# More products of ones before norms and inside linear attention, and an earlier first mask, in a twelve-sublayer decoder

## The chip, the core and the metric

The kernel runs on one core of one Trainium2 chip. The metric is device microseconds of one execution. Three executions of the kernel before took 899.19, 896.45 and 893.0 us; their median is 896.45 us.

## What is computed

The reference is a decoder of four layers on x (16 sequences of 64 tokens, 128 features, so 1024 tokens) with a context of the same shape. Each layer has a self-mixing sublayer, a cross attention to the context and a feed-forward sublayer, and each sublayer ends with its input added and a layer norm:

```
x = _layernorm(x + _L0_attn_ref(x, ...))     # linear attention
x = _layernorm(x + _L0_xattn_ref(ctx, x, ctx, mask_BxSx1_ff1, ...))
x = _layernorm(x + _L0_ffn_ref(x, ...))      # local attention and a gated net, twice
x = _layernorm(x + _L1_attn_ref(x, ...))
x = _layernorm(x + _L1_xattn_ref(x, ctx, ctx, ...))
x = _layernorm(x + _L1_ffn_ref(x, ...))      # a net, scaled by two weights
x = _layernorm(x + _L2_attn_ref(x, ...))     # the recurrence
...                                          # xattn, switch; attn, xattn, top-2 experts
```

Linear attention, the first sublayer, makes q, k, v and two gates w and r for 16 heads of 8 features, norms q and k to unit length, and sums over the 64 places s of a sequence's *batch* axis (its input counts the axis of 16 as places and the axis of 64 as batch):

```
A   = einsum('sbnq,sbnv->bnvq', k, v * w)
out = einsum('sbnq,bnvq->sbnv', q, A) * r    # then a projection
```

The recurrence mixes each token with the one before it, projects, applies relu, and runs state = state * decay + h along the 64 tokens, then projects again:

```
inp = mix * x + (1 - mix) * shifted
h = relu(inp @ W_in.T + b_in)
state = state * decay + h                    # along the tokens
out = state @ W_out.T + b_out
```

The mask of the first cross attention lets a query attend to a key only if both have a nonzero entry in mask_BxSx1_ff1.

## The kernel before

All activations stay on the chip. The 1024 tokens are two halves of 512 (h = 0 and 1), each held twice: `xt` with tokens on partitions (4 tiles of 128 by 128), for sums and norms, and `x` with features on partitions (128 by 512), for projections. Names of tiles carry the sublayer: la (linear attention), xa (every cross attention), lb (local attention), at (self attention), sf (the net of layer 1), rc (the recurrence), sw and tt (the experts).

*Order.* The source is written as Python generators: `first_stream(h)` strings the sublayers from the first cross attention (tag xa0) to the third (xa2) together, and `side_by_side` takes turns between half 0, which leads by five steps, and half 1. What the source records is then ordered by a scheduler in the tile layer, which writes one fixed list for each engine; an engine works through its list in order and waits on semaphores. So an instruction that waits holds all behind it on its engine, and the position of an instruction can differ from its place in the source.

*Buffers.* PSUM has a pool of two tiles of two banks (`psc`, tag sc, for scores and la_a) and a pool of four one-bank tiles (`pt`, tag t) for everything else: projections (la_ps, xa_pq, rc_p), transposes (la_o, xa_pt, px), outputs (po, xa_av). A new tile of a tag takes the buffer of the fourth tile before it and must wait until that one's readers are done. SBUF work tiles come from `buf(kb, ...)`, rings of 8 tiles of 2 KB, 7 of 4 KB and 4 of 8 KB per partition.

*Products of ones.* `keep_busy(out)` (L156) multiplies a 128x128 tile of ones in bf16 with 512 columns of ones into a PSUM tile which the next real product overwrites. It has no other effect on the result. It already stands 12 times before the first projection, once before most projections and transposes, four times in the norms of linear attention, six times in local attention, eight times in half 1 of xa2 and xa3.

*Linear attention* (L280 and on). The tokens are taken in eight groups of 128, in four pairs. `front(pair)` projects (la_ps: L286 and the bias rows L293), squares q and k (ACT L297), makes the gates (ACT L302), sums the squares (DVE L298) and takes the inverse root in a chain of small DVE steps (`inverse_root`, L772 to L781). `back(pair)` scales q, k and v into la_four (DVE L314), spreads v (POOL L321), transposes q (PE L333 into la_o, copied by ACT L334), forms k times v (PE L327 into la_a), masks it to its heads (DVE L329 into la_am), multiplies with q (PE L339), copies (ACT L346), transposes back (PE L348) and copies into la_att (ACT L351). front(1) is recorded before back(0), front(2) before back(1), and so on. `project_close` then makes the output projection po_la, adds the residual and calls `close`.

*Norms.* `close` makes the statistics on DVE (L195, L197), the inverse deviation in two POOL steps (L201, L204), the normed xt on DVE (L206), and returns a `flip`, which, when the stream calls it, transposes xt by PE (L224, or L235 for xa0) into px and has ACT copy it to x (L226). Its `ones` says how many products of ones the flip puts in front of its transposes.

*First cross attention.* Keys are masked by POOL (xa_km, L441), base_xa is the residual with the output's bias (POOL L685, L688), scores are PE L480, and where there is a mask, an extra product adds it to the scores (PE L491). Then follow the maximum (DVE L536), the subtraction (DVE L537), the exponent (ACT L540), transposes (PE L551) and the product with the values (PE L572). The mask tile is made by `mask_outer`: two DMAs on SP (L704) bring the mask (mo_m), POOL multiplies it (L709), DVE turns it into large negative numbers in bf16 (mo_b, L710). `attention` makes it when it first needs it:

```
        if mask and tag not in self.masks:
            self.masks[tag] = mask(work)
```

*Net and recurrence.* `sorted_ffn` runs its net for half 0 alone (half 1 only gets the second norm), and `recurrence(h)` makes the mixed input (DVE L1127, L1128), the projection rc_p (PE L151 through `group`), relu (ACT L1134), the scan (DVE L1137), the output projection po_rc (PE L151), the sum (DVE L1144) and the norm. DMA loads are issued by SP in order; w7 and w4, the weights of later cross attentions, are loaded into the places of weights that PE must have finished with.

Of the kernel before, what the change touches and what calls it, by code (L numbers as in the profile page):

```python
# [37 lines left out]
class Kernel:  # L38
# [227 lines left out]
    def linear_attention(self):  # L266


        nc, work, psc, pt = self.nc, self.aw, self.psc, self.pt
        att = self.buf(4, [N], "la_att")  # L270
        att_b = att.rearrange("p (s b j) -> p s b j", b=S // 2, j=2)
        blk8 = self.g("blk8").unsqueeze(1).to_broadcast([P, 8, P])
        pos4 = self.g("pos4").unsqueeze(2).to_broadcast([P, 4, P])

        def front(pair):
            ss = work.tile([P, 2, 32], F32, tag="la_ss", name=f"la_ss{pair}")
            made = []
            for i in range(2):
                gr = pair * 2 + i
                ps = self.psum(pt, f"la_ps{gr}")  # L280

                for _ in range(12 if gr == 0 else 1):
                    self.keep_busy(ps)
                w = self.g("L0a_w")
                n = w.shape[1]
                nc.tensor.matmul(  # L286
                    ps[:, :n], self.x_all[:, bass.ts(gr, P)], w, start=True, stop=False
                )

                rows = [self.la_b] if pair == 0 else la_b3  # L290
                ones = self.g("one") if pair == 0 else self.ones_b
                for row in rows:
                    nc.tensor.matmul(  # L293
                        ps[:, :n], ones[0:1, :], row, start=False, stop=row is rows[-1]
                    )
                sq = self.buf(2, [HALF], f"la_sq{gr}")
                nc.scalar.activation(sq[:, 0:256], ps[:, 0:256], AF.Square)  # L297
                nc.vector.tensor_reduce(  # L298
                    ss[:, i, :], sq[:, 0:256].rearrange("p (n d) -> p n d", d=8), AX.X, ALU.add
                )  # L300
                gates = work.tile([P, 32], F32, tag="la_g", name=f"la_g{gr}", bufs=4)
                nc.scalar.activation(gates, ps[:, 384:416], AF.Sigmoid)  # L302
                made.append((ps, sq, gates))
            return made, self.inverse_root(work, ss.rearrange("p i n -> p (i n)"), f"la_{pair}")

        def back(pair, made, rs):
            for i, (ps, sq, gates) in enumerate(made):
                gr = pair * 2 + i
                four = self.buf(2, [4, P], f"la_four{gr}")
                rq = work.tile([P, 16], F32, tag="la_rq", name=f"la_rq{gr}")  # L310
                nc.vector.tensor_tensor(rq, rs[:, i * 32 : i * 32 + 16], gates[:, 16:32], ALU.mult)
                factors = (rq, rs[:, i * 32 + 16 : i * 32 + 32], gates[:, 0:16])
                for n, by in enumerate(factors):
                    nc.vector.tensor_tensor(  # L314
                        four[:, n, :].rearrange("p (h d) -> p h d", d=8),
                        ps[:, bass.ts(n, P)].rearrange("p (h d) -> p h d", d=8),
                        by.unsqueeze(2).to_broadcast([P, 16, 8]),
                        ALU.mult,
                    )
                vm = sq.rearrange("p (i d) -> p i d", d=P)  # L320
                nc.gpsimd.tensor_tensor(  # L321
                    vm, four[:, 2, :].unsqueeze(1).to_broadcast([P, 4, P]), pos4, ALU.mult
                )
                a = psc.tile([P, 2, HALF], F32, tag="sc", name=f"la_a{gr}")
                for t in range(2):
                    r = slice(64 * t, 64 * t + 64)
                    nc.tensor.matmul(a[:, t, :], four[r, 1, :], sq[r, :], start=True, stop=True)  # L327
                am = self.buf(4, [8, P], f"la_am{gr}")
                nc.vector.tensor_tensor(  # L329
                    am, a.rearrange("p t (i d) -> p (t i) d", d=P), blk8, ALU.mult  # L330
                )
                po = pt.tile([P, 4, P], F32, tag="t", name=f"la_o{gr}")
                nc.tensor.transpose(po[:, 0, :], four[:, 0, :], self.g("ident"))  # L333
                nc.scalar.copy(four[:, 3, :], po[:, 0, :])  # L334

                for m in range(2):
                    for j in range(4):
                        at = (m * 4 + j) // 2 * 32
                        nc.tensor.matmul(  # L339
                            po[32 * j : 32 * j + 32, 1 + m, :],  # L340
                            four[:, 3, at : at + 32],
                            am[:, m * 4 + j, :],
                            start=True,
                            stop=True,
                        )
                nc.scalar.copy(four[:, 0:2, :], po[:, 1:3, :])  # L346
                for m in range(2):
                    nc.tensor.transpose(po[:, 1 + m, :], four[:, m, :], self.g("ident"))  # L348
                to = po[:, 1:3, :].rearrange("p m (a b) -> p m a b", b=64)
                for j in range(2):  # L350
                    nc.scalar.copy(  # L351
                        att_b[:, :, gr * 4 : gr * 4 + 4, j].rearrange("p s (m a) -> p m a s", m=2),
                        to[:, :, :, 48 * j : 48 * j + 16],
                    )
        fronts = [front(0)]
        la_b3 = []
        rows3 = self.lbp.tile([P, 2080], F32, tag="v0", name="la_b3").bitcast(BF16)
        for i in range(3):
            row = rows3[0:1, bass.ts(i, 416)]
            nc.vector.tensor_copy(row, self.la_b)  # L360
            if i < 2:
                nc.vector.tensor_tensor(self.la_b, self.la_b, row, ALU.subtract)
            la_b3.append(row)
        for pair in range(4):
            if pair < 3:
                fronts.append(front(pair + 1))
            back(pair, *fronts[pair])
        return self.project_close(pt, self.g("L0a_wo"), att, "L0a_bo", "la")


# [37 lines left out]
    def attention(  # L408
        self, h, tag, kv, hd, scale, wq, wk, wv, wo, bq=None, bk=None, bv=None, bo=None,
# [4 lines left out]
        work, psc, pt = self.aw, self.psc, self.pt  # L414
# [206 lines left out]
        if wo is not None:  # L621
# [5 lines left out]
            y = self.new_y(tag, h)  # L627
# [6 lines left out]
            else:  # L634
                nc.vector.tensor_tensor(y, ps, base, ALU.add)

        ones = 8 if h == 1 and tag in ("xa2", "xa3") else 1
        flip = self.close(pt, h, y, tag, shift=tag == "xa0", ones=ones)
        yield "last"
        flip()  # L640
# [434 lines left out]
    def sorted_ffn(self, h):  # L1075
# [30 lines left out]
        for i in range(4):  # L1106
            nc.vector.scalar_tensor_tensor(
                y[:, i, :], acc[:, i, :], ws[:, i : i + 1], self.xt[h][:, i, :], ALU.mult, ALU.add
            )
        flip = self.close(pt, h, y, "sf")  # L1110
        yield "last"
        flip()

# [1 line left out]
    def recurrence(self, h):  # L1115
        nc, pt, sc = self.nc, self.pt, self.scalars
        yield
        base = self.base(h, "rc_bout", "rc")
        rest = self.aw.tile([P, 1], F32, tag="rest", name=f"rc_rest{h}", bufs=2)
        nc.vector.tensor_scalar(rest, sc[:, 1:2], -1.0, 1.0, ALU.mult, ALU.add)  # L1120
        dec = self.buf(2, [8, S], f"rc_dec{h}")
        nc.gpsimd.memset(dec, 1.0)
        nc.gpsimd.memset(dec[:, :, 0:1], 0.0)
        nc.gpsimd.tensor_scalar(dec, dec, sc[:, 0:1], 1.0, ALU.mult, ALU.mult)
        inp = self.buf(2, [8, S], f"rc_inp{h}")
        x3 = self.x[h].rearrange("p (b s) -> p b s", s=S)
        nc.vector.tensor_scalar(inp, x3, sc[:, 1:2], None, ALU.mult)  # L1127
        nc.vector.scalar_tensor_tensor(  # L1128
            inp[:, :, 1:S], x3[:, :, 0 : S - 1], rest, inp[:, :, 1:S], ALU.mult, ALU.add
        )  # L1130
        ps = self.psum(pt, f"rc_p{h}")
        self.group(ps, [(self.g("rc_win"), inp.rearrange("p b s -> p (b s)"))])
        hid = self.buf(2, [HALF], f"rc_hid{h}")
        nc.scalar.activation(hid, ps, AF.Relu, bias=self.g("rc_bin"))  # L1134
        yield
        st = self.buf(2, [HALF], f"rc_st{h}")
        nc.vector.tensor_tensor_scan(  # L1137
            st, dec.rearrange("p b s -> p (b s)"), hid, 0.0, ALU.mult, ALU.add
        )
        ps = pt.tile([P, 4, D], F32, tag="t", name=f"po_rc{h}")  # L1140
        for i in range(4):
            self.group(ps[:, i, :], [(st[:, bass.ts(i, P)], self.g("rc_wout"))])
        y = self.new_y("rc", h)
        nc.vector.tensor_tensor(y, ps, base, ALU.add)  # L1144
        flip = self.close(pt, h, y, "rc")
        yield "last"
        flip()

# [846 lines left out]
```

## Time and profile before

| what | value |
|---|---|
| median of three executions | 896.45 us (893.0 to 899.19) |
| the profiled execution | 892.14 us |
| its span, first to last instruction | 890.4 us |
| mean TensorE clock granted | 0.893 of full |
| PE busy | 737.5 us, 83% of the span |
| PE weight loads, beside PE | 467.7 us, 53% |
| DVE busy | 493.2 us, 55% |
| ACT busy | 361.7 us, 41% |
| POOL busy | 264.8 us, 30% |
| products of ones of 512 columns into xa_pt, mean | 390 ns each, 80 of them |

Busy time is the sum of an engine's instructions; matmuls are pipelined, so that a row of them takes less than its number times the mean. The second part of the page cuts the span into 40 equal slices and gives each engine's busy share in tenths, and as PEclk the clock that TensorE was granted, where 9 is full or nearly so. The order in time gives each instruction's start, its duration, its engine and line, what it writes and reads, and in brackets how long the engine had stood idle and what ended that.

### The profile page before, as it was taken

What the parts mean: (1) busy time and instruction counts of PE and PEld (TensorE: products, weight loads), DVE (VectorE), ACT (ScalarE), POOL (GpSimd) and SP (SyncE); (2) the same over time, 40 slices, a digit from 0 to 9 for tenths busy, and PEclk for the clock granted to TensorE, in tenths of its full rate; (3) what the DMA queues carried; (4) which work ended last, traced back from release to release, by engine and by line L of the source; (5) the groups of instructions that cost most, each with busy time, mean ns of one, the idle gap of its engine ahead of it and who ended that gap; (6) DMA issues with size and microseconds to landing.
All of it is one profiled execution on the core that took longest, in us unless ns stands there. A gap on an engine that the chain in (4) does not pass through costs nothing.

```text
span 890.4 us, 17664 instructions
## 1 busy us (share of the span) xinstructions
PE 737.5 (83%) x7145; PEld 467.7 (53%) x7147; DVE 493.2 (55%) x1126; ACT 361.7 (41%) x602; POOL 264.8 (30%) x299
## 2 busy tenths in 40 slices
PE   6777888878777889789978999869767999968990
PEld 2334546455554556457564577536444565735770
DVE  4565466564846656364536575445444456665663
ACT  2223456355455534364713365323215434512320
POOL 2323143260615321212025300146151011017732
PEclk7878989899999999899977899969968799968995
DMA  7700000000000000500000000152106632021102
GB/s 278 242 13 13 1 1 2 13 1 2 1 1 1 2 1 1 190 2 1 1 1 1 1 3 1 43 134 71 49 22 190 190 115 76 14 107 51 54 25 80
DMA packets 35543, 44.43 MB, mean 50 GB/s; under 512 B 7732, under 2 KB 27445, under 8 KB 34824
## 3 DMA queue, kind: packets, MB, share of 16 engines
q1 hardware_dynamic: 33000, 38.26, 13.6%
q0 software_dynamic: 2464, 5.05, 2.0%
q8 instruction: 58, 0.95, 0.4%
q14 instruction: 21, 0.17, 0.1%
HBM read 34.51 MB, written 11.80 MB: 52 GB/s over the span
## 4 chain that ended last, share of the span: by engine, by line
PE 54%; DVE 18%; POOL 7%; ACT 5%; issue 4%; DMA 3%; SPq 1%; DVEq 0%; POOLq 0%; ACTq 0%
PE xa_sc L480 4%; PE xa_av L572 4%; PE xa_pt L551 3%; PE tt_py L151 3%; PE sw_pe L151 3%; PE tt_ph L151 2%; PE at_sc L480 2%; DVE lb_t L818 2%; PE lb_qk L151 2%; DVE lb_t L832 2%; PE at_av L572 2%; PE xa_sc L491 2%; PE at_pt L551 2%; PE xa_pt L156 1%; PE lb_pw L151 1%
## 5 line engine op out<-in xcount | busy, mean ns | idle before, releaser
L536 DVE TENSOR_REDUCE xa_mx<-xa_sc 128x16 f32<-128x1024 f32 x40 | 48.7, 1219 | 63.8 <-PE xa_sc L491 41.3
L838 POOL TENSOR_TENSOR lb_t<-lb_t,lb_t 128x1024 f32<-128x1024 f32 x16 | 37.7, 2357 | 99.4 <-DVE lb_t L832 95.2
L554 ACT COPY xa_eT<-xa_pt 128x512 f32<-128x512 f32 x80 | 45.5, 587 | 40.8 <-PE xa_pt L551 40.0
L540 ACT ACTIVATE xa_e<-xa_e 128x1024 f32<-128x1024 f32 x40 | 42.3, 1058 | 37.6 <-DVE xa_e L537 37.5
L480 PE MATMUL xa_sc<-xa_km,xa_q 32*64 32x256 f32 x640 | 55.2, 404 | 0.7 <-ACT xa_q L431 0.5
L441 POOL TENSOR_SCALAR xa_km<-xa_k,const 128x512 f32<-128x512 f32 x40 | 27.0, 695 | 82.5 <-ACT xa_k L429 49.1
L551 PE MATMUL xa_pt<-const,xa_e 128*128 128x128 f32 x320 | 48.8, 280 | 1.8 <-ACT xa_e L540 1.8
L537 DVE TENSOR_TENSOR xa_e<-xa_sc,xa_mx 128x1024 f32<-128x1024 f32 x40 | 48.7, 1218 | 2.1
L551 PEld LDWEIGHTS xa_pt<-const,xa_e 128*128 128x128 f32 x320 | 40.3, 145 | 13.1 <-ACT xa_e L540 3.7
L572 PEld LDWEIGHTS xa_av<-v,xa_eT 128*64 128x64 f32 x1280 | 40.5, 138 | 8.2 <-issue 6.1
L572 PE MATMUL xa_av<-v,xa_eT 128*64 128x18 f32 (+1 forms) x1280 | 44.2, 209 | 0.0
L156 PEld LDWEIGHTS <-ones_b 128*128 128x128 bf16 x255 | 25.3, 106 | 35.9 <-issue 19.8
L151 PE MATMUL lb_qk<-w,lb_hs 128*128 128x512 f32 x64 | 35.8, 686 | 8.5 <-DVE lb_t L832 4.8
L480 PEld LDWEIGHTS xa_sc<-xa_km,xa_q 32*64 32x64 f32 x640 | 24.7, 136 | 19.9 <-issue 12.8
L201 POOL TENSOR_TENSOR rstd_xa<-mv_xa,eps 128x4 f32<-128x4 f32 x8 | 1.6, 200 | 112.2 <-DVE mv_xa L197 112.2
L814 DVE TENSOR_REDUCE lb_ss<-lb_t 128x16 f32<-128x1024 f32 x16 | 19.5, 1217 | 27.9 <-ACT lb_t L811 27.9
L156 PE MATMUL xa_pt<-ones_b 128*128 128x512 bf16 x80 | 30.2, 390 | 0.0
L862 POOL TENSOR_TENSOR lb_t<-lb_t,lb_rs 128x1024 f32<-128x1024 f32 x16 | 30.1, 1902 | 0.0
L1610 POOL DMA_INDIRECT tt_out<-tt_ys,tt_outs x23 | 22.5, 976 | 18.6 <-DVE tt_ys L1609 16.2
L868 PE MATMUL lb_pf<-const,lb_t 128*128 128x128 f32 x128 | 20.1, 312 | 9.4 <-POOL lb_t L862 9.3
L480 PE MATMUL at_sc<-at_km,at_q 32*64 32x256 f32 x256 | 22.5, 446 | 6.0 <-DVE at_rel L533 4.5
L151 PE MATMUL sw_pe<-sw_gu,sw_xs 128*128 x46 | 26.7, 665 | 0.0
(471 smaller groups left out, 1762.9 us busy)
## 6 DMA issues: line engine op xcount, KB each, us to landing
sw_gu<-in_sw_gu SPq DMA_DIRECT2D x4, 1024.0 KB, 6.8
at_mem<-at_rsb SPq DMA_DIRECT2D x16, 256.0 KB, 2.7
at_rel<-at_mem SPq DMA_DIRECT2D x32, 128.0 KB, 2.9
w<-in_w SPq DMA_DIRECT2D x1, 3114.0 KB, 13.7
sw_dn<-in_sw_dn SPq DMA_DIRECT2D x4, 512.0 KB, 7.0
tt_w<-in_tt_w SPq DMA_DIRECT2D x2, 1024.0 KB, 8.0
tt_b<-in_tt_b SPq DMA_DIRECT2D x1, 2048.0 KB, 7.4
sw_in<-in_zeros SPq DMA_DIRECT2D x1, 1472.0 KB, 11.2
```

Of the source, the lines that this page charges most:

```text
L151: self.nc.tensor.matmul(out, lhsT, rhs, start=n == 0, stop=n == len(pairs) - 1)
L156: self.nc.tensor.matmul(out, self.ones_b, self.ones_b.unsqueeze(1).to_broadcast([P, 4, P]), start=True, stop=True)
L441: nc.gpsimd.tensor_scalar(kms[-1][:, i % 4, :], k, hm[:, i : i + 1], 1.0, ALU.mult, ALU.mult)
L480: nc.tensor.matmul(sc[64 * j : 64 * j + 64, gg, at : at + 256], q[r, t], part[r, :, t] if local else part[r, :, :], start=not masked or (p ...
L536: nc.vector.tensor_reduce(mx, scored, AX.X, ALU.max)
L537: nc.vector.tensor_tensor(e3, scored, mx.unsqueeze(2).to_broadcast([P, 16, S]), ALU.subtract)
L540: nc.scalar.activation(e3, e3, AF.Exp, scale=scale)
L551: nc.tensor.transpose(ps[:, bass.ts(n, P)], blocks[:, bass.ts(n, P)], self.g("ident"))
L554: nc.scalar.copy(eT[:, gg, :], ps)
L572: nc.tensor.matmul(av[64 * j : 64 * j + 64, pr, hp, :, :], eT[:, gg, at : at + 64], v[:, b, hp, :, :], start=True, stop=True,)
L838: nc.gpsimd.tensor_tensor(t1, t1, t2.rearrange("p t n d -> p t (n d)"), ALU.add)
L862: nc.gpsimd.tensor_tensor(t3, t3, rs[:, bass.ts(r, 16)].unsqueeze(2).to_broadcast([P, 16, 64]), ALU.mult)
```

## The change

Products of ones are added in five places, and one call is moved.

- In `back`, before the transpose into la_o: ten in the first group of the first pair, four in the first group of the other pairs, two in the second group of each pair. They are written into the la_o tile.
- The flip of xa0 in half 0 gets four instead of one.
- The flip of sf in half 0 gets four instead of none (`close` in half 1 of `sorted_ffn` is another call and stays at none).
- In the recurrence, before the projection rc_p and before po_rc: six each in half 0, three each in half 1.
- The flip of rc gets four instead of none in both halves.
- `mask_outer` for xa0 is called at the end of the four pairs of linear attention, ahead of `project_close`, instead of in the attention. Its two DMAs, its POOL product and its DVE step go with it. Its tile comes from the ring of 2 KB tiles, so it takes another place in that ring.

```diff
                 po = pt.tile([P, 4, P], F32, tag="t", name=f"la_o{gr}")
+
+                for _ in range((10 if pair == 0 else 4) if i == 0 else 2):
+                    self.keep_busy(po.rearrange("p n m -> p (n m)"))
                 nc.tensor.transpose(po[:, 0, :], four[:, 0, :], self.g("ident"))
...
             back(pair, *fronts[pair])
+
+        self.masks["xa0"] = self.mask_outer(work)
         return self.project_close(pt, self.g("L0a_wo"), att, "L0a_bo", "la")
...
-        ones = 8 if h == 1 and tag in ("xa2", "xa3") else 1
+        ones = 8 if h == 1 and tag in ("xa2", "xa3") else 4 if h == 0 and tag == "xa0" else 1
...
-        flip = self.close(pt, h, y, "sf")
+        flip = self.close(pt, h, y, "sf", ones=4)
...
         ps = self.psum(pt, f"rc_p{h}")
+        for _ in range(6 - 3 * h):
+            self.keep_busy(ps)
         self.group(ps, [(self.g("rc_win"), inp.rearrange("p b s -> p (b s)"))])
...
         ps = pt.tile([P, 4, D], F32, tag="t", name=f"po_rc{h}")
+        for _ in range(6 - 3 * h):
+            self.keep_busy(ps.rearrange("p i d -> p (i d)"))
         for i in range(4):
...
-        flip = self.close(pt, h, y, "rc")
+        flip = self.close(pt, h, y, "rc", ones=4)
```

The change can be built without being run, and the built lists show where the scheduler puts things. In linear attention the ten products stand directly ahead of the first L333; in the later pairs three of the four stand ahead of L327 and one behind it, and in the last pair the two parts of a group's L327 are pulled apart by other products. The POOL step of the mask stands behind the last L321, its DVE step between the last two L329, its DMAs ahead of the load of w7. Around the recurrence of half 0 the lists of PE, DVE and POOL change in order as well: the keys' projection xa_pk and the end of half 1's previous cross attention stand between rc_p and po_rc, and seven of POOL's eight xa_km stand before the inverse deviation of rc, where before it was one.

## The prediction

> **What bounds the kernel now.** I read the busy row and the clock row of the page first, since the change only adds work to TensorE. PE is busy 83% of the span, but the clock row falls under full speed again and again, and the chain that ended last is 54% PE.
>
> ```profile
> ## 2 busy tenths in 40 slices
> PE   6777888878777889789978999869767999968990
> ...
> PEclk7878989899999999899977899969968799968995
> ```
>
> Then I took the clock in 1 us steps. It has two values, 1.00 and 0.50, and changes only at instants 3.413 us apart (10.46, 24.12, 34.36, 37.78, 48.0, 58.26, 78.74, 85.56, 457.62, 467.86 us and so on, all at 0.23 us past a multiple). The table of stages shows the slow stretches in the regions that the change touches; behind the comma stands PE busy, and PEclk is the column before the DMA share.
>
> ```profile
> 10.46:24.11 13.65, 7.60 (x18) 2.62 (x17) 10.54 (x43) 1.59 (x8) 2.40 (x3) 0.50 0.95 352
> 48.01:58.25 10.24, 9.17 (x49) 4.10 (x51) 6.24 (x19) 2.21 (x9) 2.43 (x3) 0.50 0.00 1
> 74.34:77.74 3.40, 0.01 (x2) 0.03 (x1) 0.97 (x4) 1.21 (x1) 2.26 (x2) 1.00 0.01 2
> 78.73:85.56 6.83, 6.83 (x40) 3.07 (x33) 5.51 (x5) 2.26 (x3) 0.00 (x0) 0.50 0.01 2
> 457.62:467.86 10.24, 5.85 (x14) 3.21 (x14) 4.27 (x10) 1.27 (x2) 3.37 (x3) 0.50 0.00 1
> 471.27:478.10 6.83, 6.47 (x39) 3.50 (x39) 3.96 (x13) 1.02 (x2) 6.83 (x11) 0.50 0.00 0
> 501.99:508.82 6.83, 6.57 (x45) 3.48 (x49) 1.88 (x4) 3.59 (x5) 2.69 (x4) 0.50 0.00 0
> ```
>
> Last came the order of time. In these lines: start, duration, instruction; in brackets the idle time ahead of it and its releaser. First the start of linear attention, then the mask, then the recurrence.
>
> ```profile
> 18.64 0.29 DVE L314 TENSOR_TENSOR la_four<-la_ps,la_g 128x128 f32<-128x128 f32 x1
> 19.08 0.45 PE L333 MATMUL la_o<-const,la_four 128*128 128x128 f32 x1 [4.05 <-DVE la_root L781]
> 21.25 3.39 PE L327 MATMUL la_a<-la_sq,la_four 64*128 64x512 f32 x8
> 23.38 2.54 DVE L329 TENSOR_TENSOR la_am<-la_a,const 128x1024 f32<-128x1024 f32 x2 [1.02 <-PE la_a L327]
> ...
> 74.97 1.26 POOL L688 TENSOR_TENSOR base_xa<-base_xa,xt_la 128x512 f32<-128x512 f32 x1 [1.23 <-DVE xt_la L206]
> 76.19 1.04 POOL L709 TENSOR_TENSOR mo_m<-mo_m,cols 128x512 f32<-128x512 f32 x1
> 77.74 0.59 PE L491 MATMUL xa_sc<-mo_b,ident_b 128*128 128x512 bf16 x2 [3.40 <-DVE mo_b L710]
> 80.59 1.06 PE L156 MATMUL xa_pt<-ones_b 128*128 128x512 bf16 x2
> ...
> 460.05 2.05 PE L151 MATMUL rc_p<-rc_inp,w 128*128 128x512 f32 x2 [2.35 <-issue]
> 464.13 2.08 PE L151 MATMUL po_rc<-w,rc_st 128*128 128x128 f32 x8 [2.04 <-DVE rc_st L1137]
> 489.85 1.12 PE L151 MATMUL rc_p<-rc_inp,w 128*128 128x512 f32 x2
> 493.82 1.16 PE L151 MATMUL po_rc<-w,rc_st 128*128 128x128 f32 x8
> ```
>
> The reader is to see three things. PE waits 4.05 us for the first transpose of linear attention. PE stands 3.40 us before the first mask product, because POOL's L709 stands behind two base_xa steps, and the clock then halves for 6.83 us. And the same recurrence product takes 2.05 us in half 0 and 1.12 us in half 1.
>
> **What the Trainium skill says.** "TensorE: Matmul & The Clock Gate", section "Part 1: The HAM clock gate", says that a free-running window of 3413 ns decides between half and full clock, and that idle halves it. The trace agrees: steps of 3.413 us, values 0.50 and 1.00. The same page, "HAM oscillation", asks for no idle gap over about 3.4 us; here a full-speed window that is 0.59 to 0.68 busy sometimes fell (454.2 to 457.6, 0.68) and sometimes not (65.1 to 68.5, 0.59), so I treat about half as the edge. Its "Part 4: PE-mode transpose" says that transposes don't count as busy in the same way, which fits the fall at 457.6 after a window with four transposes.
>
> **Prices.** One product of ones costs 0.216 us at full clock (four took 1.03 with 0.38 for the last: 0.65/3) and 0.43 at half (two took 1.06, the last 0.63). The change adds 30 in linear attention (10+2, then three times 4+2), 3 for xa0, 4 for sf, 12+6+8 for the recurrence: 63.
>
> **Part 1, the mask.** In the built order of the changed kernel its POOL product stands right after the last L321, where POOL idles (9.23 us before 64.59), its DVE step between the last two L329, and its two DMAs (3.4 us from issue to landing) on SP ahead of the loads of w7 and w4, which wait for PE; POOL's base_xa and norm steps are passed only by 1.04 us that ends before their inputs are there. All of that is covered; without the cover it would cost 1.04+0.43. What goes is the stall: L491 can start when the scores end, at 74.34, not 77.74. Next late are DVE and ACT: maximum from 75.0 (DVE has xt_la until 74.9), subtraction to 77.5, exponent 78.6, transposes at full clock from 79.25, second exponent and the copies after it, and the first xa_av at 82.35 against 87.50. That is 5.1 us: 3.4 of stall and 1.7 of half clock. PE is full until 104, so it lasts. I take 4.9 (3.4 to 5.3).
>
> **Part 2, ones in linear attention.** la_o takes the buffer of the first la_ps, since four buffers hold la_ps 0 to 3, so its ten ones can't run in the 4.05 us gap: they start with the wait's end, 19.08, after the L314 of 18.64 has freed it, and at half clock. 10x0.43 = 4.3, to 23.35; transpose 0.45; two ones and a transpose at about full clock 0.8; la_a from 24.6 in place of 21.25, but at full clock 0.9 instead of 1.7 before the first L329, which moves from 23.38 to about 25.6: +2.2. A window that falls otherwise gives 1.6 to 3.1. DVE, ACT and the next projections wait behind it in order, so it is not absorbed. In pairs 1 and 2 the four ones fit PE's waits (1.13 before 32.94, 1.19 and 0.86 around 45.5), and L329 is bound by DVE's root steps, so a faster la_a gains nothing there; the two ones before the next transpose stand ahead of L348 and cost about 0.3. In pairs 2 and 3 full clock instead of the 10.24 us at half would bring the last L329 2.4 us forward, but the order now puts the second la_a product of the last group behind L339 of the group before, which gives 1.4 back, and ones ahead of its transpose another 0.4: -0.6. Sum +2.2+0.3-0.6 = +1.9; if the clock falls again there, +1 more. I take +2.2 (bounds: -3.2, the clock gains of 0.85 and 2.4 with all ones covered; and +12.8, all 30 at 0.43 on the path).
>
> **Part 3, xa0.** Two of the extra ones run before the transposes at 107.7, one or two in the gap after 108.8. lb_qk at 113.79 runs at half clock (3.4 before ACT, 1.7 at full), but the 2.5 us idle just before it stays. I take a quarter of 1.7: -0.4 (0 to -1.7).
>
> **Part 4, sf and recurrence.** In half 0 the ones of sf and rc_p fill 454.5 to 458, the six of po_rc 459.2 to 460.5, so both windows are full and the clock stays. But the order also splits xa_av: its second half now comes after px_sf, and DVE's reciprocal of it stands before L1128, so rc_inp ends 0.6 later. rc_p 460.65 to 461.75 (before 462.10), scan to 463.75, po_rc to 464.95 (before 466.2). Then seven xa_km of POOL stand before the norm of rc, which ends 470.4 as before (470.7); but xt_rc no longer runs beside them, 1.11 us in place of 2.73, and x_rc comes 2.4 us sooner. There the ones don't help: PE idles from 468.8, and the projection may run at half clock again. Scores start 2.3 to 2.7 sooner. In half 1, three ones per product lie in full PE time, 6x0.216 = +1.3, against half clock at 484.93 and 501.99 (6.57 busy, up to 3 us); four ones of px_rc lie in idle time. Following the order to half 1's scores I get 3.9 to 4.5 sooner, less what a new fall takes. I take -4.0 (-1 to -6). From there to 568 PE is full, so it lasts.
>
> **Sum.** -4.9+2.2-0.4-4.0 = -7.1. The profiled execution took 892.14 us (span 890.4, 1.7 around it): 885.0. It lies 4.3 under the median of 896.45; as the windows run free, it is one draw among others, so I subtract from the mean of the four executions, 895.2, and get 888.1.
>
> **Rivals.** (A) the sum, 888.1, own range 884 to 892. (B) Linear attention gains too: its slow stretches go and the ones are covered, -3.2 instead of +2.2: -12.5, 882.7. For: 13.65 and 10.24 us at half clock; against: the buffer wait. (C) The recurrence is throttled anyway, since its waits for POOL and DVE are longer than the ones: part 4 is 0, 892.1. For: norms of 2 us with no PE work; against: full windows at 454 to 461. (D) Slower: the products of ones in linear attention stay on the path at half clock. Their wait for a buffer is the mechanism, 0.43 each the price, and from 22 of 30 (9.4 us) they eat the other parts' 9.3; all 30 give -9.3+12.8 = +3.5, 898.7. For: ten surely wait so; against: pairs 1 and 2 have gaps.
>
> **Chances.** A 0.57, B 0.20, C 0.17, D 0.06. A measurement of this kernel tells about 1% from no change, here 9 us: faster means under 887.5. B and under half of A are there: 0.44. Same: 0.53. Slower than 905.4 needs D and bad windows: 0.03. The range takes in most of B and all of C's middle: 881.5 to 895.5.
>
> **What would show it.** The mask: no wait of PE before its L491, and full clock after 75. Linear attention: ten ones from about 19 at 0.43 and the first L329 at 25 to 26; po_la about 2 us later than 62.62. Recurrence: rc_p and po_rc of half 0 at 1.1 us. I'd be wrong if the ten ones start before 19, if the clock falls again at 75 to 86 or 455 to 468, or if another wait holds half 1 while half 0 gains.

## The result, and the profile after

The changed kernel takes 889.77 us (median of 20 executions, 880.88 to 900.39), the kernel before 894.2 us (20 executions, 887.45 to 902.0). The ratio is 0.9938, with a 95% interval of 0.9913 to 0.9963: 5.5 us faster (3.3 to 7.8). That is clear of no change, but under the 1% (9 us) that the forecast had set as the edge between "same" and "faster". The ratio is formed from the executions that lie no more than 1.5% above the fastest of their kernel (17 of the 20 of the changed one), so it differs from that of the two medians, 0.995. The profiled execution took 890.40 us (span 888.6).

The page of the changed kernel, with the rows that were shown of before:

```profile
## 2 busy tenths in 40 slices
PE   7878898788687889799989899779767999968990
...
PEclk9999989989999989899996999979877879957995
```

The clock row is better in the first third and around the middle, but not in the last third, where nothing was changed.

The table of stages of the changed kernel (us, then PE busy, PEld, DVE, ACT, POOL; then PEclk, DMA share, GB/s), cut at the instants where the clock changes:

```profile
16.88:20.30 3.42, 2.94 (x7) 1.05 (x8) 3.35 (x12) 0.00 (x0) 2.15 (x2) 0.50 0.98 422
20.30:33.94 13.64, 10.11 (x69) 4.48 (x69) 5.66 (x15) 2.98 (x12) 5.19 (x7) 1.00 1.02 356
...
45.19:63.53 18.34, 14.10 (x104) 5.44 (x103) 10.90 (x28) 4.03 (x16) 5.12 (x5) 1.00 0.07 16
71.50:74.91 3.41, 3.41 (x26) 1.79 (x27) 0.89 (x8) 0.71 (x2) 2.60 (x4) 0.50 0.00 0
...
78.32:109.04 30.72, 26.93 (x318) 17.19 (x316) 17.90 (x32) 15.30 (x24) 3.91 (x6) 1.00 0.01 1
...
467.44:481.10 13.66, 12.83 (x54) 4.88 (x53) 9.11 (x24) 3.50 (x5) 6.22 (x9) 0.50 0.00 1
481.10:508.00 26.90, 24.15 (x283) 15.33 (x283) 15.97 (x26) 12.01 (x19) 7.75 (x11) 1.00 0.01 2
```

And the order of time: linear attention, the mask, the recurrence. The line numbers of the changed kernel are 3 higher than those of before from the ones in `back` on, and 5 higher behind the mask's call.

```profile
17.36 3.75 PE L156 MATMUL la_o<-ones_b 128*128 128x512 bf16 x10 [4.20 <-DVE la_root L786]
22.87 2.35 DVE L329 TENSOR_TENSOR la_am<-la_a,const 128x1024 f32<-128x1024 f32 x2 [2.22 <-PE la_a L327]
55.12 1.04 POOL L714 TENSOR_TENSOR mo_m<-mo_m,cols 128x512 f32<-128x512 f32 x1
56.80 1.23 DVE L329 TENSOR_TENSOR la_am<-la_a,const 128x1024 f32<-128x1024 f32 x1 [3.22 <-PE la_a L327]
57.94 0.42 DVE L715 TENSOR_SCALAR mo_b<-mo_m 128x512 bf16<-128x512 f32 x1
60.13 1.22 DVE L329 TENSOR_TENSOR la_am<-la_a,const 128x1024 f32<-128x1024 f32 x1 [1.77 <-PE la_a L327]
63.53 2.05 PE L151 MATMUL po_la<-w,la_att 128*128 128x128 f32 x16 [0.47 <-ACT la_att L354]
76.71 0.60 PE L496 MATMUL xa_sc<-mo_b,ident_b 128*128 128x512 bf16 x2
...
456.49 1.02 PE L151 MATMUL rc_p<-rc_inp,w 128*128 128x512 f32 x2
459.55 1.16 PE L151 MATMUL po_rc<-w,rc_st 128*128 128x128 f32 x8 [0.52 <-DVE rc_st L1144]
466.62 0.59 PE L224 MATMUL px_rc<-const,xt_rc 128*128 128x128 f32 x2 [2.76 <-DVE xt_rc L206]
468.58 2.08 PE L151 MATMUL xa_pq<-x_rc,w 128*128 128x512 f32 x2 [0.73 <-ACT x_rc L226]
483.54 1.02 PE L151 MATMUL rc_p<-rc_inp,w 128*128 128x512 f32 x2
487.71 1.05 PE L151 MATMUL po_rc<-w,rc_st 128*128 128x128 f32 x8
```

The reader is to see four things. The ten ones wait 4.20 us, just as the transpose did before (4.05): they did not fill that gap. The first mask product at 76.71 has no idle time in brackets, and the clock stays full from 74.91 to 109.04. The last two L329 stand apart, at 56.80 and 60.13, where before they ran back to back. And rc_p and po_rc of half 0 are at full clock, but the clock halves right after, from 467.44 to 481.10, behind a wait of 2.76 us for the norm. The last two L329 of the kernel before:

```profile
57.71 2.45 DVE L329 TENSOR_TENSOR la_am<-la_a,const 128x1024 f32<-128x1024 f32 x2 [3.73 <-PE la_a L327]
```

A whole single trace can't give the 5.5 us: from the first sw_pe to the first y_tt, code that the change does not touch, this trace takes 284.4 us and that of before 279.2. So traces are compared below by stage, and times by many executions.

### The profile page after: what moved, and what is told of

It is laid out like the page before. It is cut to its first block, busy times and chain, and to the rows that moved or that the text cites. A ratio compares the mean times of both kernels' runs of the same rounds, so it can differ in the third digit from the quotient of the medians.

```text
span 888.6 us, 17788 instructions
## 1 busy us (share of the span) xinstructions
PE 744.9 (84%) x7210; PEld 470.0 (53%) x7210; DVE 490.8 (55%) x1126; ACT 360.6 (41%) x602; POOL 266.2 (30%) x299
## 3 DMA queue, kind: packets, MB, share of 16 engines
q1 hardware_dynamic: 33000, 38.26, 13.7%
## 4 chain that ended last, share of the span: by engine, by line
PE 55%; DVE 18%; POOL 6%; ACT 5%; issue 4%; DMA 3%; SPq 1%; POOLq 0%; DVEq 0%; ACTq 0%
PE xa_sc L485 5%; PE xa_av L577 4%; PE xa_pt L556 3%; PE tt_py L151 3%; PE sw_pe L151 3%; PE tt_ph L151 2%; PE lb_qk L151 2%; PE at_sc L485 2%; PE xa_sc L496 2%; DVE lb_t L823 2%; DVE lb_t L837 2%; PE at_av L577 2%; PE xa_pt L156 1%; PE at_pt L556 1%; POOL xa_km L446 1%
## 5 line engine op out<-in xcount | busy, mean ns | idle before, releaser
L156 PEld LDWEIGHTS <-ones_b 128*128 128x128 bf16 x318 | 31.4, 107 | 52.7 <-issue 32.9
L1342 POOL DMA_INDIRECT sw_got<-sw_in,sw_ids x23 | 22.1, 962 | 15.3 <-DVE sw_ids L1322 6.1
```

The lines of the kernel that those rows point to most:

```text
L156: self.nc.tensor.matmul(out, self.ones_b, self.ones_b.unsqueeze(1).to_broadcast([P, 4, P]), start=True, stop=True)
```

## The experiments

Eleven runs were made, of ten kernels (one of them twice), all timed. A ratio is to the kernel before on the same chip. Four distances from each kernel's trace are used, each in us:

- *la*: from the end of the wait ahead of the first la_o to the first L329, and from the first la_o of pair 2 to po_la. Pairs are counted from 0, so pair 2 is the third and pair 3 the last.
- *mask*: from po_la to the first y_xa, the sum after the first attention of half 0.
- *recurrence*: from the first y_sf to the first sw_pe, so the recurrence of both halves and the cross attention around and after it.

| kernel | first L329 | pair 2 to po_la | mask | recurrence | ratio (95%) |
|---|---|---|---|---|---|
| before | 4.30 | 17.11 | 42.47 | 143.23 | 1 |
| mask only | 4.30 | 15.08 | 38.43 | 143.58 | 0.9906 (0.9877 to 0.9936) |
| linear attention only | 6.49 | 18.35 | 49.71 | 143.64 | 1.0067 (1.0040 to 1.0095) |
| sf and recurrence only | 4.31 | 15.82 | 40.40 | 140.27 | 0.9946 (0.9922 to 0.9970) |
| changed kernel | 5.51 | 18.34 | 38.45 | 140.18 | 0.9938 (0.9913 to 0.9963) |
| it, without ones in linear attention | 4.30 | 15.00 | 38.46 | 140.20 | 0.9837 (0.9787 to 0.9888) |
| the same again | 4.30 | 17.12 | 36.93 | 143.34 | 0.9888 (0.9848 to 0.9927) |
| with the ten alone | 6.41 | 15.00 | 36.93 | 140.24 | 0.9937 (0.9913 to 0.9961) |
| with the 20 others alone | 4.30 | 18.34 | 38.44 | 140.07 | 0.9920 (0.9894 to 0.9945) |
| with the last pair's six alone | 4.30 | 15.23 | 38.42 | 140.14 | 0.9898 (0.9840 to 0.9955) |
| the ten in the score buffer, no others | 3.21 | 17.53 | 37.80 | 143.32 | 0.9851 (0.9825 to 0.9877) |

The last pair's six, and the two last kernels of this section, ran on a chip on which the kernel before took 909.76 us in place of 894 to 895; only their ratios and stages are used.

**The mask alone.**

```diff
+        self.masks["xa0"] = self.mask_outer(work)
         return self.project_close(pt, self.g("L0a_wo"), att, "L0a_bo", "la")
```

> The kernel before with the mask's call moved and no product of ones added. My theory (part 1): the wait of PE ahead of the first mask product goes and the clock no longer falls right after it, -4.9 us (3.4 to 5.3), so a ratio of about 0.9945; in the order of time L491 stands right behind the first scores with no wait. Rival: the softmax behind it (DVE, ACT) or the two DMAs, now ahead of w7 and w4, take the wait's place, 0 to -1.5 us, ratio 0.9985 to 1.000.

Measured: 0.9906, 8.4 us faster (5.7 to 11.0), more than either side expected. The stage says why. With the mask moved, po_la to y_xa takes 36.9 to 38.5 us in every trace; with the mask late, 40.40, 42.47 and 49.71 us. PE's wait before the mask product is in all three of these, 3.40 us in the trace of before, 0.72 us in that with sf and recurrence only and 1.89 us in that with linear attention only; what varies more is the clock after it. In the table of stages of the kernel with ones in linear attention only, where the mask stays late, around its L494, the mask product:

```profile
78.28:81.70 3.42, 1.53 (x19) 0.70 (x18) 0.69 (x3) 1.89 (x2) 2.26 (x2) 1.00 0.02 7
81.70:105.58 23.88, 23.84 (x160) 14.43 (x158) 10.58 (x10) 8.47 (x12) 0.00 (x0) 0.50 0.00 1
```

The window with the wait is 1.53 of 3.42 us busy, the clock falls, and it stays at half for 23.88 us, seven windows, though PE is busy for 23.84 of them. In the trace of before, on which the prediction rests, it was down for two windows (6.83 us). In the kernel with sf and recurrence only the clock was low ahead of the scores (67.82 to 74.64), so that the wait left was 0.72 us, and it did not fall after it. So the stage is 2 to 11 us longer with the late mask than the 38.4 us that it mostly takes with the early one, by what the clock did. That it is the place of the 3.41 us windows that decides this is a reading of three traces; no run tested it alone.

**Ones in linear attention alone.**

```diff
+                for _ in range((10 if pair == 0 else 4) if i == 0 else 2):
+                    self.keep_busy(po.rearrange("p n m -> p (n m)"))
```

> The kernel before with the 30 products of ones in linear attention alone. My theory (part 2): ten ones wait for the buffer and lie on the path at half clock, +2.2 us (window draws 1.6 to 3.1), ratio about 1.0025; po_la about 2 us later, counted from the end of the wait ahead of the ten. Rival B: the slow stretches of linear attention go and the ones are covered, -3.2 us, ratio 0.9964. Rival D: all 30 stay on the path at half clock, up to +12.8 us, ratio 1.014.

Measured: 1.0067, 6.0 us slower (3.6 to 8.5). My sign, but outside the range that I gave; rival B is refuted. The first L329 comes 6.49 us after the wait's end against 4.30, the predicted 2.2. The rest has to be elsewhere.

**Ones of sf and the recurrence alone.**

```diff
-        flip = self.close(pt, h, y, "sf")
+        flip = self.close(pt, h, y, "sf", ones=4)
...
+        for _ in range(6 - 3 * h):
+            self.keep_busy(ps)
...
+        for _ in range(6 - 3 * h):
+            self.keep_busy(ps.rearrange("p i d -> p (i d)"))
...
-        flip = self.close(pt, h, y, "rc")
+        flip = self.close(pt, h, y, "rc", ones=4)
```

> The kernel before with only the products of ones of sf, rc_p, po_rc and rc. My theory (part 4): -4.0 us (-1 to -6), ratio about 0.9955, with rc_p and po_rc of half 0 at 1.1 us. Rival C: the recurrence is throttled anyway and the norm of half 0 ends no sooner, 0 us, ratio 1.000, half 1's scores start when they did. The trace of the changed kernel, counted from the first sum of sf, shows half 1's scores only 2.0 us sooner, so I now lean to -2 to -3.

Measured: 0.9946, 4.8 us faster (2.7 to 7.0), with rc_p and po_rc of half 0 at full clock. In the stage, 140.1 to 140.3 us with these ones against 143.2 to 143.6 without: 3.3 us, in six of the eight traces in the table that have them. The clock falls behind them in all eight, at 464 to 470 us; in the six it is back after 13.7 us, in the two others (143.3) only after 20.5 us, and the gain is gone. In those two executions the outcome is rival C's.

**The changed kernel without ones in linear attention, twice.** The edit takes the two lines above out.

> The changed kernel without the 30 products of ones in linear attention, so mask, xa0, sf and recurrence alone. My theory: parts 1, 3 and 4 without the +2.2, -9.3 us by the prediction, ratio 0.9896, about 2 us faster than the changed kernel. Rival B: these ones are a gain of 3.2, so this kernel is 3 us slower than the changed one, ratio about 0.997.

> The changed kernel without the 30 products of ones in linear attention, once more, since six executions stood behind the first figure: ratio 0.984 to 0.989 if the stage's cost read from the traces (about 2 to 4 us) is all that they cost, 0.979 to 0.984 if they cost the 7 to 9 us that the two runs with and without them gave.

Measured: 0.9837 from six executions and 0.9888 from fourteen. With the interval of the first so wide, the two agree; both lie below the changed kernel's 0.9938, by 1.0 and 0.5%, 9 and 4.5 us. Rival B, by which this kernel is the slower one, is refuted. The second figure lies at the upper end of the range for a cost of 2 to 4 us, and its interval touches that of the changed kernel, so by these two runs the cost may still be near the predicted 2.2 us; the run with these ones alone (3.6 to 8.5) puts it above.

**The ten alone.**

```diff
-                for _ in range((10 if pair == 0 else 4) if i == 0 else 2):
+                for _ in range(10 if gr == 0 else 0):
```

> The changed kernel with only the ten products of ones of the first pair left in linear attention; its instructions stand, apart from them, in the order of the kernel without any. Theory (the ten wait for the buffer and lie on the path): first L329 5.5 to 6.5 us after the end of the wait ahead of them, against 4.30 without; the rest of the stage as without ones, so +1 to +2 us over the changed kernel without ones, ratio to the kernel before about 0.986 to 0.991. Rival (the cost sits in the 20 others and in the order that they bring): nothing over the changed kernel without ones, even a gain from a full clock, ratio about 0.983.

Measured: 0.9937, above what either side gave. In the order of time of this kernel:

```profile
19.27 4.43 PE L156 MATMUL la_o<-ones_b 128*128 128x512 bf16 x10 [4.03 <-DVE la_root L786]
23.49 0.64 PE L336 MATMUL la_o<-const,la_four 128*128 128x128 f32 x2
```

They wait 4.03 us for the buffer, then take 4.43 us at half clock, and the transpose that started at the wait's end without them starts 4.2 us later. The first L329 moves by only 2.1 us: without the ten, the second transpose waits another 1.35 us for DVE, and L327 runs at half clock behind it. After that nothing in this trace is later than without ones (15.00 us from pair 2 to po_la), so the trace shows 2 us, while the time is 4.4 us (against 0.9888) or more above that without ones.

**The 20 others alone.**

```diff
+                for _ in range(0 if pair == 0 else 4 if i == 0 else 2):
```

> The changed kernel with the 20 products of ones of the later three pairs left in linear attention and the ten of the first pair taken out; PE's order is that of the changed kernel. Rival (the order, with the two parts of the last group's L327 pulled apart, costs whatever the clock): from pair 2's first la_o to po_la 18.3 us as in the two traces with all 30, against 15.0 to 17.1 in the four without; +2.6 us over the changed kernel without ones, ratio about 0.987. Theory as it was predicted (the later pairs give -0.3): ratio about 0.983.

Measured: 0.9920, 4.5 us above what the rival gave, and 18.34 us from pair 2 to po_la, to 0.01 us that of the two kernels with all 30. The last two L329 of this kernel, and po_la:

```profile
56.20 1.22 DVE L329 TENSOR_TENSOR la_am<-la_a,const 128x1024 f32<-128x1024 f32 x1 [3.23 <-PE la_a L327]
59.53 1.23 DVE L329 TENSOR_TENSOR la_am<-la_a,const 128x1024 f32<-128x1024 f32 x1 [1.77 <-PE la_a L327]
62.93 2.05 PE L151 MATMUL po_la<-w,la_att 128*128 128x128 f32 x16 [0.47 <-ACT la_att L354]
```

and the same in the changed kernel without ones in linear attention:

```profile
59.45 2.13 PE L327 MATMUL la_a<-la_sq,la_four 64*128 64x512 f32 x8
60.63 2.36 DVE L329 TENSOR_TENSOR la_am<-la_a,const 128x1024 f32<-128x1024 f32 x2 [1.61 <-PE la_a L327]
65.54 0.71 PE L151 MATMUL po_la<-w,la_att 128*128 128x128 f32 x4 [0.47 <-ACT la_att L351]
```

With the 20, the second L329 starts 3.33 us after the first, having waited for L327; without, it starts right behind the first, 1.18 us after it (2.36 us for both). That makes 2.15 us. Another 1.4 us arise ahead of the first of the two: from the start of the last pair's L327 to this L329 it is 2.58 us with the 20 and 1.18 us without. L327 has two parts for each group, one for each half of the partitions. In the trace with the 20, a group of pair 2 and the first part of a group of pair 3:

```profile
45.77 1.13 PE L327 MATMUL la_a<-la_sq,la_four 64*128 64x512 f32 x4 [0.38 <-POOL la_sq L321]
53.62 1.12 PE L327 MATMUL la_a<-la_sq,la_four 64*128 64x512 f32 x2 [0.30 <-POOL la_sq L321]
```

Four records (both parts) take 1.13 us where they stand together, and two records (one part alone) take 1.12 us. So two parts that stand together run beside one another, and parts pulled apart are each paid in full. In this order the parts are pulled apart in both groups of the last pair, at 53.62 and 55.04 and at 56.74 and 58.37, and not only in its last group. From the start of this L327 to po_la it is 9.31 us with the 20 and 6.09 us without. The clock is full in both stretches, as it is in the changed kernel (45.19 to 63.53 in the table of stages). So here are 3.2 us that have nothing to do with the clock.

**Only the last pair's six.**

```diff
+                for _ in range((4 if i == 0 else 2) if pair == 3 else 0):
```

> The changed kernel with only the six products of ones of the last pair left in linear attention. In this build the two parts of the last group's L327 stand together again. Theory (the 18.3 us from pair 2's first la_o to po_la come from the order, in which the last L329 waits for a part of L327 that stands behind the back end of the group before): 15.0 to 17.1 us as without ones, plus at most 0.5. Rival (the six products themselves and what they hold up cost it): 17.5 to 18.4 us. In the time, theory: ratio to the kernel before about 0.987; rival: about 0.990.

In this build both parts of the last group's L327 stand in front of the back end of the group before it. Measured: 15.23 us, in the order of time:

```profile
50.91 0.47 PE L336 MATMUL la_o<-const,la_four 128*128 128x128 f32 x1 [1.19 <-DVE la_four L314]
61.02 1.23 DVE L329 TENSOR_TENSOR la_am<-la_a,const 128x1024 f32<-128x1024 f32 x1 [1.64 <-PE la_a L327]
62.51 1.23 DVE L329 TENSOR_TENSOR la_am<-la_a,const 128x1024 f32<-128x1024 f32 x1 [0.27 <-PE la_a L327]
66.14 2.05 PE L151 MATMUL po_la<-w,la_att 128*128 128x128 f32 x16 [0.47 <-ACT la_att L354]
```

The same six products stand in the last pair, each L327 has its parts together, and the two L329 start 1.49 us apart. So in the traces it is the order that costs the 3 us, and the ones only through the order that comes with them. This kernel also lacks the 14 ones of pairs 0 to 2, and its profiled execution is the slowest of its six (910.41 us). The time, 0.9898 (0.9840 to 0.9955), can't tell the theory's 0.987 from the rival's 0.990.

**The ten in the score buffer.** They are written into la_a, which nobody uses yet, and the later pairs have none.

```diff
                 a = psc.tile([P, 2, HALF], F32, tag="sc", name=f"la_a{gr}")
+                for _ in range(10 if gr == 0 else 0):
+                    self.keep_busy(a[:, 0, :])
```

> The changed kernel, with the ten products of ones of the first pair written into the free score buffer of la_a in place of la_o, and none in the later pairs. Theory (it is the buffer that puts the ten on the path): they run inside the 4 us gap ahead of the first transpose, the first L329 comes 4.3 to 4.6 us after the end of la_root's chain as without ones, and the windows of the gap count as busy: at least as fast as the changed kernel without ones, ratio 0.983 or less. Rival (ten more products cost their time wherever they stand): +2 to +4 us, ratio 0.986 to 0.988.

Measured: 0.9851 (0.9825 to 0.9877), 13.3 us faster than before and, with 881.24 us (median of 22), the fastest of the kernels that have a narrow interval. In its order of time:

```profile
13.37 2.33 PE L156 MATMUL la_a<-ones_b 128*128 128x512 bf16 x10
17.66 0.30 PE L335 MATMUL la_o<-const,la_four 128*128 128x128 f32 x1 [1.96 <-DVE la_root L785]
20.87 1.23 DVE L331 TENSOR_TENSOR la_am<-la_a,const 128x1024 f32<-128x1024 f32 x1
```

Now the ten run in the gap, and at full clock (2.33 us), the wait left is 1.96 us, and the first L329 comes 3.21 us after it (3.2 to 3.8 in the three traces with this edit), against 4.30 without ones and 5.5 to 6.5 with them in la_o. Same work, other buffer: the buffer's wait was what put the ten on the path. In the source the kernel with the ten alone differs from this one only in that buffer, and it takes 0.9937 against 0.9851, 7.7 us more, where the first L329 differs by 3.2 us. The ratio itself lies between those of the theory (0.983 or less) and of the rival (0.986 or more). Whether this kernel is faster than the one without any ones there (0.9837 and 0.9888) can't be told.

**21 ones in front of rc's transposes in half 0**, where PE waits 2.76 us, on top of the kernel with the score buffer.

```diff
-        flip = self.close(pt, h, y, "rc", ones=4)
+        flip = self.close(pt, h, y, "rc", ones=21 if h == 0 else 4)
```

> The kernel with the ten products of ones in the score buffer, and 21 in place of four before the transposes of rc in half 0, where PE waits 2.76 us for the norm. Theory (that wait lets the clock fall at 464 to 467 us, and the fall is why the recurrence gains 3 us and not more): no fall between 460 and 475, projection xa_pq and the first scores at full clock (1.1 and 1.0 us in place of 2.08 and 2.00), from the first sum of sf to sw_pe 137 to 139 us in place of 140.2 to 143.3, ratio about 0.981. Rival (the score products with their 32 rows, or the waits behind, let it fall anyway, or DVE bounds these steps): 140 to 143.5 us, ratio 0.985 or more.

Measured: 0.9912, 147.63 us for the stage: 4.3 us more than in the kernel it was made from, and 0.6% (5.5 us) more in the time. In its order of time:

```profile
456.83 4.70 PE L156 MATMUL px_rc<-ones_b 128*128 128x512 bf16 x21
462.25 1.10 PE L224 MATMUL px_rc<-const,xt_rc 128*128 128x128 f32 x4 [0.73 <-DVE xt_rc L206]
464.10 1.12 PE L151 MATMUL xa_pq<-x_rc,w 128*128 128x512 f32 x2
466.20 1.11 PE L484 MATMUL xa_sc<-xa_km,xa_q 32*64 32x256 f32 x16
474.24 1.97 PE L555 MATMUL xa_pt<-const,xa_e 128*128 128x128 f32 x8 [2.92 <-ACT xa_e L544]
```

The first half of the theory holds in the main: no fall until 473.50 (I had said none before 475), projection 1.12 us in place of 2.08, scores 1.11 in place of 2.00. The second fails: PE then stands 2.92 us for the softmax, the clock falls at 473.50 for 13.66 us instead, and the build's order changes with the ones: half 1's po_rc now stands behind more scores, transposes and value products, 9.5 us after its rc_p (478.88 to 488.39), where it was 5.5 us in the kernel with the score buffer. The fall has moved and the order is worse; which of the two costs more was not told apart.

**Without the ones of the recurrence in half 1**, again from the kernel with the score buffer.

```diff
-        for _ in range(6 - 3 * h):
+        for _ in range(6 if h == 0 else 0):
```

> The kernel with the ten products of ones in the score buffer, and without the three and three products of ones in the recurrence of half 1 (the six and six of half 0 stay). By the prediction these six cost 1.3 us of full PE time and save half clock at 485 and 502. Theory: the clock is full there anyway once half 0's fall is over, so without them 1 us faster, from the first sum of sf to sw_pe 139 to 142 us. Rival: without them the clock falls again at 485 to 510, 2 to 3 us slower.

Measured: 0.9883 (0.9829 to 0.9937, six executions), 143.41 us, against 143.32 with them. In both traces the long fall (20.5 and 23.9 us, from 464.40 and 462.90 on) covers the place that these ones were to protect. Neither theory is shown; what they do in an execution with the short fall was not seen.

## Why the forecast of the time held, and which steps did not

The time was forecast at 888.1 and is 889.77, in the range and on the side of "same"; the change was forecast at -7.1 us and is -5.5. That it came so close was luck: two terms of the sum were wrong by 3.5 to 4 us each, with opposite signs, and cancelled. The three parts run alone give -8.4 +6.0 -4.8 = -7.2, and the changed kernel -5.5 (-7.8 to -3.3), so they add up, within their intervals.

**Part 1, the mask: mechanism right, size too small.** Forecast -4.9 (3.4 to 5.3), measured -8.4 (5.7 to 11.0). No wait at the mask product and full clock behind it, as predicted. The mis-sized term is "1.7 of half clock": I took the fall of one profiled execution, two windows, for the price. The fall can last seven. Against that one trace the stage gained 4.0 to 5.5 us, as forecast. Over all traces the stage moves from 40.4 to 49.7 (mean of three traces 44.2) to 36.9 to 38.5, about 6 us by the traces, of which the stall itself is at most the predicted 3.4.

**Part 2, linear attention: the first step right, the third wrong.** That the ten wait for the buffer and go to the path is shown by two runs: in la_o they move the first L329 back by 1.2 to 2.2 us (forecast 2.2), in another buffer forward by 0.6 to 1.1. The step that failed is "pairs 2 and 3": full clock was to bring the last L329 2.4 us forward, the split L327 to give 1.4 back and the ones 0.4, sum -0.6. In each of the three traces that have the split order the last L329 starts 3.3 us after the one before it, and pair 2 to po_la takes 18.3 us. That is 3.3 us more than the shortest traces without it, and 2.3 us more than their mean (15.0 to 17.5 us in the table, mean 16.0), which includes what the clock took from some of them. I had seen the split in the built order, but only that of the last group, and priced it as one product's delay. It is in both groups of the last pair; each part of L327 then takes the 1.12 us that both took together, and the last L329 waits for the back end of the group before (L342 there) as well. Both terms together make about 4 us in the traces. The clock gives some of it back in some executions: two traces with no ones in the first pairs spent 30.7 us of this stage at half clock (14.14 to 44.86 in the kernel with the mask alone), and took 32.5 us from the wait's end to pair 2, against 27.8 to 29.2 with the ten in la_o and 26.4 to 26.5 in the best without. The timed cost, 4.5 to 9 us by three comparisons, is mostly higher than the traces' stages give, and in the time the two terms don't add up: 0.9937 with the ten alone, 0.9920 with the 20 others alone, 0.9938 with all 30. What makes up the rest stays open: one profiled execution for each kernel is too few to say how often each fall happens.

**Part 3, xa0.** Forecast -0.4; no trace shows a difference. From the first y_xa to the first y_lb it is 209.9 to 213.1 us with these ones in nine traces, 209.9 to 213.6 without them in four. It wasn't run alone.

**Part 4, the recurrence: right, with two causes in it.** Forecast -4.0 (-1 to -6), measured -4.8 (-2.7 to -7.0), 3.3 us in the traces. rc_p is at 1.02 and po_rc at 1.16 us. xt_rc of half 0 takes 1.11 us in place of 2.73, now that POOL's xa_km run ahead of it; before, then changed:

```profile
470.76 2.73 DVE L206 TENSOR_SCALAR xt_rc<-y_rc,mv_rc,rstd_rc 128x128 f32<-128x128 f32 x4 [2.26 <-POOL rstd_rc L204]
466.22 1.11 DVE L206 TENSOR_SCALAR xt_rc<-y_rc,mv_rc,rstd_rc 128x128 f32<-128x128 f32 x4 [2.30 <-POOL rstd_rc L204]
```

In half 1 L206 still runs beside them and still takes 2.73 us. That fits the Trainium skill, "SBUF — State Buffer", section "SBUF: two separate sides", which says that GpSimd and a DVE instruction that uses the second pair of ports hold this pair as an exclusive lock, so that the later of the two blocks. That L206 is such an instruction is inferred from its times; the trace doesn't say it. Counted from the first y_sf, the sum y_rc of half 0 comes 1.7 us sooner than before, xt_rc starts only 0.6 us sooner, as the seven xa_km now stand ahead of its norm, and the projection xa_pq starts 3.1 us sooner, of which the shorter xt_rc makes 1.6. So a good part of the gain is the new order and not the clock. No run has the one without the other. That the projection "may run at half clock again" came true at 467.44: I had named a fall at 455 to 468 as a sign against me, and it came at that edge, after the recurrence's products and not among them.

**The rivals.** B is refuted (+6.0 where it said -3.2). C's outcome is that of two traces out of eight. D had the right mechanism and place, and more of it than I gave it: not 0.43 us for each of 30 products, but about 2 us for ten of them and 2 to 3 for the order that the others brought.

**Half as the edge.** I took a window that is about half busy as the edge for a fall, from windows of the trace of before. The Trainium skill's "HAM oscillation" in "TensorE: Matmul & The Clock Gate" asks only for no idle gap over about 3.4 us. Here the clock fell behind the mask's window, 1.53 of 3.42 us busy, whose longest gap was 1.89 us, so shorter gaps are enough. No single busy share is the edge: before, a window with 2.33 of 3.42 us busy was followed by a fall and one with 2.00 of 3.41 was not. For the way up the busy share didn't serve either: windows of scores (32 rows), transposes and value products stayed at half clock while PE was busy 23.84 of 23.88 us.

## What to carry to other kernels

Products of ones are only free where their output buffer is free when the gap opens: ask which reader frees the buffer, since the same ten products cost 2 us in one PSUM tile and gained up to 1 us in another. Added products can bring real work into another order; compare the built order around every group that was touched, and price a split by what no longer overlaps, here the two parts of one product and the chain behind them, not as the delay of one instruction. Price a stall that lets the clock fall from several traces, or as a span, as the fall lasted two windows behind a mask wait of 3.40 us and seven behind one of 1.89 us in another trace, with the same products behind it, for a reason that stays open.

## What the runs showed of the hardware that I had not expected

- How long a fall lasts. All falls last a whole number of windows of 3.41 us, the length that the Trainium skill gives in "TensorE: Matmul & The Clock Gate", "Part 1: The HAM clock gate". But behind the wait for the mask the clock came back after 6.83 us in one trace and 23.88 us in another, with PE busy throughout in both.
- Two parts of one product. The two parts of L327, on the two halves of the partitions, took 1.13 us standing together and 1.12 us for one alone.
- Late in the kernel, on code that the change does not touch, single traces ahead of the last three kernels differ by 9 us (275.2 to 284.4 from sw_pe to y_tt), and the last three, on another chip, took 293 to 302 us there. That is more than any part of this change, so a trace shows where time goes, and only many executions show how much.
